# A two-layer product-quantised convolution block: where the sorts, the second image's preparation and the last image's pieces are placed

## The chip, the cores and the metric

The kernel runs on one core of a Trainium2 chip. A core has five engines, each with its own instruction stream: TensorE (PE, matrix multiplication, with weight loads listed as PEld), VectorE (DVE), ScalarE (ACT), GpSimd (POOL) and SyncE (SP, which here only issues DMA transfers; GpSimd issues transfers too). TensorE writes to PSUM, of which a partition has eight banks of 512 float32 numbers; the other engines work on SBUF, and VectorE and ScalarE also read PSUM. The metric is the time of one execution on the device, in microseconds (us); less is better.

## The reference

Sixteen images of 256 channels and 28 x 28 pixels go through one residual block. Each of its two convolutions is replaced by a soft lookup: for each channel the 3 x 3 neighbourhood of a pixel is compared with 16 codes, a softmax over the distances gives weights, and the weighted codes are multiplied by the convolution's weights.

```python
def amm_conv3x3(x, centroids, w_sub):
    patches = conv_general_dilated_patches(x, (3, 3), (1, 1), 'SAME')
    p = patches.reshape(B, C, s, Ho * Wo).transpose(0, 3, 1, 2)     # s = 9 taps
    d = sum(p * p, -1)[..., None] - 2.0 * einsum('bncs,cks->bnck', p, centroids) + sum(centroids ** 2, -1)
    attn = softmax(-d, axis=-1)                                      # k = 16 codes
    lut = einsum('cks,cso->cko', centroids, w_sub)
    return einsum('bnck,cko->bno', attn, lut)

xn = group_norm(x)                       # 32 groups
out = relu(bn1(amm_conv3x3(xn, centroids1, wsub1)))
out = bn2(amm_conv3x3(out, centroids2, wsub2))
out = out * sigmoid(relu(mean(out) @ w1 + b1) @ w2 + b2)             # squeeze and excitation
return x + relu(out + xn)
```

## The kernel before

**The pipeline.** An image takes two stages, one for each layer; the stages of neighbouring images are interleaved: (layer 0, image 0), (0, 1), (1, 0), (0, 2), (1, 1) and so on. A stage has 16 slots: two pixel tiles of 384 and 400 pixels (PXT), and for each 8 groups of channels. In a slot four steps of different groups run, each group passing through them slot by slot:

```python
patches(u, tile)   # SyncE: 4 DMAs, patch rows from DRAM (pat) to a tile pt, three slots ahead
logits(u)          # TensorE: 16 small matmuls into two pairs of PSUM banks
b_exp(u)           # ScalarE: exp of the logits, pair -> e
b_num(u)           # TensorE: 16 small matmuls, numerators and sum, e -> two pairs of banks
b_turn(u)          # VectorE: two 32x32 transposes pair -> nt, reciprocal of the sum
c_scale(u)         # GpSimd: numerators times reciprocal, nt -> k
c_turn(u)          # VectorE: transpose k -> q
c_look(u, o, h)    # TensorE: lookups, 128x128 weights on q, accumulated in the bank acc0 or acc1
```

The lookups of a pixel tile start four slots after its logits. Logits and numerators share a ring of three pairs of PSUM banks (`pair`); the lookups own two further banks. The first lookup runs in slot 4.

```python
    ring = [p_ring.tile([P, 2, 512], F32, name=f"pair{i}") for i in range(3)]
    def pair():
        turn[0] += 1
        return ring[turn[0] % 3]
    def bank():
        return pair()[:, 0]
```

**Jobs in a slot.** Everything else is put into slots by `plan.at(slot, position, function, ...)`. Positions within a slot, in order: LOGITS, LOAD, MOVE, EXP, LOOK_A, NUM, TURN, SMALL, LOOK_B, MAX, LOOK_C, TURN_BACK, REST. Each engine executes its instructions in the order in which they are so emitted; waits between engines are put in by the framework.

**The sorts.** Channels are put in another order by matmuls with a permutation, computed at the start. The first layer's lookup weights are sorted in six parts, the second layer's codes in one call, both with banks of the ring:

```python
    def sort_ws1(i):
        t = raw[i // 2][:, i % 2]
        for j in range(PART // P):
            ps = bank()
            for b in range(NB):
                nc.tensor.matmul(ps[:, :C], lhsT=t[:, b, j * P : (j + 1) * P], rhs=perm[:, b], ...)
            # copied to ws[0] by VectorE (j == 1) or ScalarE
    def by_position(ps, rhs):
        for v in range(NB):
            for b in range(NB):
                nc.tensor.matmul(ps[:, v], lhsT=perm[:, b, v * P : (v + 1) * P], rhs=rhs[:, b], ...)
    def sort_c2():
        ps = pair()
        m0 = 0
        for d, rhs in zip(d_c2, (c2_sb, c2_less)):
            m = rhs.shape[2]
            by_position(ps[:, :, m0 : m0 + m], rhs)
            t = scratch(NB * m).rearrange("p (b m) -> p b m", b=NB)
            nc.scalar.copy(t, ps[:, :, m0 : m0 + m])
            nc.gpsimd.dma_start(view(d, 0, [[m, P], [P * m, NB], [1, m]]), t)
            m0 += m
```

**Preparing an image.** The image is loaded, its statistics are taken (`gn_stats`, VectorE, four pieces), the group means follow (`gn_mean`, `gn_var`), the normalised image goes to `ims`, two copies shifted by a pixel (dx = 0 and 2; dx = 1 is the image itself) to `sides`, and from these the patch rows are written to DRAM: `to_pat`, one DMA for a shift, a block k of channels, a half h of the partitions, and optionally one pixel tile. Groups 0 to 3 of a stage read the half h = 0, groups 4 to 7 the half h = 1.

```python
        def prep_near(self, l, pat, t):
            for i, dx in enumerate((0, 2)):
                for k in range(NB):
                    self.at(t + i, REST, shift, l, dx, k)
            step = {v: i for i, v in enumerate(STEPS)}   # STEPS: h outermost, then dx in (1, 0, 2), then k
            put = lambda s, dx, k, h, px: self.at(s, REST, to_pat, l, step[dx, k, h], pat, *PXT[px])
            if l == 0:                                   # the second image only, with t = 10
                for i in range(len(STEPS)):
                    put(t + i // 2, *STEPS[i], 0)
                late = [(dx, k, h, 1) for dx in (0, 2) for h in range(2) for k in range(NB)]
                late += [(1, k, h, 1) for h in range(2) for k in range(NB)]
                for i, v in enumerate(late):
                    put(t + 6 + i // 2, *v)
                return
        # ... (layer 1)
        def norm(self, b, t):                            # the second image: t = 9
            for n, (k, i) in enumerate((k, i) for k in range(NB) for i in range(2)):
                self.at(t - 8 + n, REST, gn_stats, b, k, i)
            self.at(t - 3, SMALL, gn_mean, b)
            self.at(t - 1, SMALL, gn_var, b)
            for k in range(NB):
                self.at(t + k, REST, gn_apply, b, k)
```

The second image (b = 1) is loaded by SyncE in slot 0. Its first-layer stage is slots 16 to 31; slots 24 to 31 use the second pixel tile.

**The last image.** After its last lookup: the squeeze and excitation gate, then for two blocks k of channels and two halves i of the pixels y = relu(y * gate + normed) + x, and the stores.

```python
        def close_last(self, b, ob, te):
            # ... se_hidden, se_gate, se_scale
            for i in range(2):
                at(gate_norm, b, 0, i)        # VectorE: y * gate + normed
                at(relu, b, 0, i)             # ScalarE
                at(residual, b, 0, i)         # GpSimd: y + x
            for i in range(2):
                at(gate_norm, b, 1, i)        # VectorE
                at(relu_residual, b, 1, i)    # VectorE: max(y, 0) + x
            at(store_part, b, ob, 1, 0)
            at(store_part, b, ob, 0, 0, 2)
            at(store_part, b, ob, 1, 1)
```

Of the kernel before, what the change touches and what calls it, by code (L numbers as in the profile page):

```python
# [8 lines left out]
F32 = mybir.dt.float32  # L9
# [63 lines left out]
def kernel(  # L73
# [58 lines left out]

    def spare():

        return ring[(turn[0] + 1) % 3][:, 1]
# [53 lines left out]
    cw = [load(cw1, "cw0"), const.tile([P, NT, 32], F32, name="cw1")]  # L189
    load_codes = lambda: nc.sync.dma_start(cw[1], cw2)  # L190
# [134 lines left out]
    def sort_ws1(i):  # L325

        t = raw[i // 2][:, i % 2]
        for j in range(PART // P):
            ps = bank()
            for b in range(NB):  # L330
                nc.tensor.matmul(  # L331
                    ps[:, :C], lhsT=t[:, b, j * P : (j + 1) * P], rhs=perm[:, b], start=(b == 0), stop=(b == NB - 1)
                )
            w = ws[0][:, i * PART // P + j]
            if j == 1:
                nc.vector.tensor_copy(w, ps[:, :C])
            else:
                nc.scalar.copy(w, ps[:, :C])
# [3 lines left out]
    def by_position(ps, rhs):  # L342
        for v in range(NB):
            for b in range(NB):
                nc.tensor.matmul(  # L345
                    ps[:, v], lhsT=perm[:, b, v * P : (v + 1) * P], rhs=rhs[:, b], start=(b == 0), stop=(b == NB - 1)
                )

    def sort_c2():

        ps = pair()
        m0 = 0
        for d, rhs in zip(d_c2, (c2_sb, c2_less)):
            m = rhs.shape[2]
            by_position(ps[:, :, m0 : m0 + m], rhs)
            t = scratch(NB * m).rearrange("p (b m) -> p b m", b=NB)
            nc.scalar.copy(t, ps[:, :, m0 : m0 + m])
            nc.gpsimd.dma_start(view(d, 0, [[m, P], [P * m, NB], [1, m]]), t)
            m0 += m
# [213 lines left out]

    def gate_norm(b, k, i):

        y, gt = ys[b][0][half(k, i)], se[b]
        im = ims[0][:, k, W + i * (HW // 2) : W + (i + 1) * (HW // 2)]
        nc.vector.scalar_tensor_tensor(y, y, gt[:, k : k + 1], im, op0=ALU.mult, op1=ALU.add)

    def store_part(b, ob, k, i, n=1):  # L580
        v = slice(i * (HW // 2), (i + n) * (HW // 2))
        nc.sync.dma_start(ob[k * P : (k + 1) * P, v], ys[b][0][:, k, v])
# [179 lines left out]
    class Plan:  # L762
# [78 lines left out]
        def prep_near(self, l, pat, t):  # L841
# [6 lines left out]
            if l == 0:  # L848
                for i in range(len(STEPS)):
                    put(t + i // 2, *STEPS[i], 0)  # L850
                late = [(dx, k, h, 1) for dx in (0, 2) for h in range(2) for k in range(NB)]
                late += [(1, k, h, 1) for h in range(2) for k in range(NB)]
                for i, v in enumerate(late):
                    put(t + 6 + i // 2, *v)
# [13 lines left out]
        def norm(self, b, t):  # L868

            for n, (k, i) in enumerate((k, i) for k in range(NB) for i in range(2)):  # L870
                self.at(t - 8 + n, REST, gn_stats, b, k, i)
# [5 lines left out]
        def close_last(self, b, ob, te):  # L877
# [4 lines left out]
            for i in range(2):  # L882
                at(gate_norm, b, 0, i)
                at(relu, b, 0, i)
                at(residual, b, 0, i)
            for i in range(2):
                at(gate_norm, b, 1, i)
                at(relu_residual, b, 1, i)
            at(store_part, b, ob, 1, 0)
            at(store_part, b, ob, 0, 0, 2)  # L890
            at(store_part, b, ob, 1, 1)
# [55 lines left out]
    for si, (l, b) in enumerate(stages):  # L947
        t = si * NS
        plan.stage(l, b, pat_of(l, b), t, () if l == 0 else MAXED)
        if l == 0 and b >= 1:  # L950
# [5 lines left out]
            plan.norm(b, n0)  # L956
# [4 lines left out]
        if l == 1:  # L961
# [7 lines left out]
            else:  # L969
                plan.at(t + NS + LC - 1, REST, watch)  # L970
                plan.at(t + NS + LC - 1, REST, nc.gpsimd.drain)
                plan.close_last(b, out[b], t + NS + LC)
    for i in range(len(STEPS) // 2, len(STEPS)):
# [7 lines left out]
    plan.at(3, REST, load_codes)  # L981
    plan.at(3, REST, sort_c2)
# [116 lines left out]
```

## Time and profile before

| | |
|---|---|
| median of 3 runs | 2724.41 us (2719.69 to 2725.13) |
| span of the profiled run | 2720.5 us, mean granted TensorE clock 0.993 |
| instructions | 90148 |
| first logits | 30.92 us |
| first lookup (slot 4) | 62.61 us |
| last lookup | ends at about 2706.2 us |
| bytes moved by DMA | 514.98 MB, mean 189 GB/s |

How to read it. The page gives, for each engine, its busy time and its share of the span; then the span in 40 slices, with the busy share of each in tenths and the clock that TensorE was granted. The timeline lists instructions in order of time: start, length, engine, line of the kernel, operation, what it writes and reads, and how many were merged; in square brackets stands how long the engine was idle before it and what ended that. SPq is the queue in which SyncE issues DMA transfers: the time of such a line is the issue, and the data lands later. In a list of waits a line names the engine that waited, what it waited for, the sum in us, how often, and the longest.

A TensorE that is busy for a whole slice does not say that it does useful work at full speed[...].

### The profile page before, as it was taken

The page shows a single profiled execution, that of the slowest core. Times are in us where ns is not written, and L with a number is a line of the kernel's source. Part 1 is how long each engine was busy: PE and PEld are TensorE (multiplying, and loading weights), DVE is VectorE, ACT ScalarE, POOL GpSimd, SP SyncE. Part 2 cuts the span into 40 slices and gives each one's busy share as a digit, 9 for nine tenths or more (in the row PEclk, how much of TensorE's full clock was granted, in tenths as well). Part 3 has the DMA queues.
Part 4 walks back from the last instruction along what each step waited for, and adds up shares of the span by engine and source line. Part 5 has one row for each costly group of instructions (what it writes and reads, how often), then busy time and mean ns, then how long its engine had stood idle before and what let it go on. Part 6 is the DMA issues. An engine that isn't in the chain of part 4 may idle for free.

```text
span 2720.5 us, 90148 instructions
## 1 busy us (share of the span) xinstructions
PE 2684.0 (99%) x37748; PEld 1080.5 (40%) x37748; DVE 2177.3 (80%) x2639; ACT 1091.8 (40%) x1591; POOL 1905.0 (70%) x2723
## 2 busy tenths in 40 slices
PE   7999999999999999999999999999999999999997
PEld 4333434344343343433434343443443434333343
DVE  4668787887878878788787888878788787878886
ACT  2333443434334343433434334343443434334332
POOL 3888676766777677676776777667776776766764
PEclk8999999999999999999999999999999999999999
DMA  8688888767678676777767778676776767775561
GB/s 233 182 222 234 223 218 218 205 175 201 173 210 211 168 198 169 209 200 185 203 174 202 185 194 215 170 201 169 212 210 172 200 169 211 194 177 127 141 166 45
DMA packets 231944, 514.98 MB, mean 189 GB/s; under 512 B 34408, under 2 KB 186088, under 8 KB 231528
## 3 DMA queue, kind: packets, MB, share of 16 engines
q0 software_dynamic: 51968, 267.09, 37.0%
q1 hardware_dynamic: 179560, 242.03, 34.1%
q8 instruction: 299, 4.90, 0.7%
q14 instruction: 117, 0.96, 0.1%
HBM read 264.64 MB, written 244.37 MB: 187 GB/s over the span
## 4 chain that ended last, share of the span: by engine, by line
PE 97%; DMA 1%; DVE 1%; issue 0%; SPq 0%; ACT 0%; DVEq 0%
PE acc L729 63%; PE pair L603 17%; PE pair L665 16%; DMA pt<-pat 1%; PE pair L331 1%; PE pair L526 0%; DMA xt<-in_x 0%; DMA pt<-in_ws 0%; DMA sort_sb<-in_sorting 0%; PE pair L453 0%; PE pair L345 0%; PE pair L464 0%; PE pair L513 0%; DVE nt L677 0%; DVE y L555 0%
## 5 line engine op out<-in xcount | busy, mean ns | idle before, releaser
L729 PE MATMUL acc<-q,ws 128*128 128x384 f32 (+1 forms) x4096 | 1630.1, 518 | 0.0
L677 DVE STREAM_TRANSPOSE nt<-pair 128x832 f32<-128x832 f32 (+1 forms) x1024 | 977.5, 992 | 480.4 <-PE pair L665 382.2
L693 POOL TENSOR_TENSOR k<-nt,rc 128x832 f32<-128x832 f32 (+1 forms) x512 | 803.9, 1570 | 775.0 <-DVE rc L683 735.9
L655 ACT ACTIVATE e<-pair 128x768 f32<-128x768 f32 (+1 forms) x960 | 738.4, 821 | 1033.0 <-PE pair L603 1031.7
L729 PEld LDWEIGHTS acc<-q,ws 128*128 128x128 f32 x4096 | 701.2, 189 | 878.3 <-issue 542.1
L603 PE MATMUL pair<-pt,wd 19*32 19x384 f32 (+1 forms) x16384 | 498.1, 501 | 8.3 <-DVE nt L677 5.8
L711 DVE STREAM_TRANSPOSE q<-k 128x832 f32<-128x832 f32 (+1 forms) x512 | 488.6, 954 | 1.8 <-POOL k L693 1.8
L665 PE MATMUL pair<-e,cw 32*32 32x384 f32 (+1 forms) x16384 | 486.5, 500 | 0.2
L683 DVE RECIPROCAL rc<-nt 128x104 f32<-128x104 f32 (+1 forms) x512 | 398.5, 778 | 17.6
L603 PEld LDWEIGHTS pair<-pt,wd 19*32 19x32 f32 x16384 | 123.4, 103 | 303.3 <-issue 229.6
L699 POOL TENSOR_TENSOR tail<-nt,rc 128x104 f32<-128x104 f32 (+1 forms) x512 | 242.3, 473 | 0.0
L665 PEld LDWEIGHTS pair<-e,cw 32*32 32x32 f32 x16384 | 120.7, 103 | 288.8 <-issue 152.8
L729 PE MATMUL acc<-qt,ws 128*128 128x400 f32 (+1 forms) x512 | 217.0, 506 | 0.0
L705 POOL TENSOR_TENSOR total<-total,nt 128x96 f32<-128x96 f32 (+1 forms) x480 | 212.1, 442 | 0.0
L498 POOL DMA_DIRECT2D pat<-side x282 | 189.8, 673 | 1.2 <-ACT side L487 0.8
L705 POOL TENSOR_TENSOR total<-total,rc 128x96 f32<-128x96 f32 (+1 forms) x480 | 187.6, 391 | 0.0
L729 PEld LDWEIGHTS acc<-qt,ws 128*128 128x128 f32 x512 | 92.0, 189 | 94.7 <-issue 41.3
L648 ACT ACTIVATE e<-e 128x768 f32<-128x768 f32 (+1 forms) x64 | 54.7, 857 | 179.3 <-DVE e L641 178.3
L633 POOL TENSOR_TENSOR z<-z,mx 128x768 f32<-128x768 f32 (+1 forms) x64 | 98.8, 1544 | 0.0
L498 POOL DMA_DIRECT2D pat<-im x140 | 95.0, 679 | 0.1
L741 ACT ACTIVATE im<-acc,bnsh,bnsc 128x384 f32<-128x384 f32 (+1 forms) x64 | 43.4, 678 | 124.2 <-PE acc L729 124.2
L751 ACT ACTIVATE y<-acc,bnsh,bnsc 128x384 f32<-128x384 f32 (+1 forms) x64 | 43.4, 677 | 88.4 <-PE acc L729 85.7
(120 smaller groups left out, 894.4 us busy)
## 6 DMA issues: line engine op xcount, KB each, us to landing
pat<-side POOLq DMA_DIRECT2D x224, 588.0 KB, 5.7
pt<-pat SPq DMA_DIRECT2D x1024, 112.5 KB
pt<-pat SPq DMA_DIRECT2D x1024, 108.0 KB
pat<-im POOLq DMA_DIRECT2D x112, 588.0 KB, 5.3
xt<-in_x POOLq DMA_DIRECT2D x30, 784.0 KB, 6.8
out_dram<-y POOLq DMA_DIRECT2D x15, 784.0 KB, 5.8
pat<-side POOLq DMA_DIRECT2D x32, 300.0 KB, 5.9
pat<-side POOLq DMA_DIRECT2D x26, 288.0 KB, 5.3
```

What stands on the lines that cost most here:

```text
L498: eng.dma_start(view(pat, (ROWS * p0 + 9 * k + 3 * dx) * HW + px, [[ROWS * HW, m], [HW, 3], [1, n]]), bass.AP(v.tensor, v.offset, [list(v. ...
L603: nc.tensor.matmul(ps[t // 2][c : c + 32, t % 2, :n], lhsT=wd[l][32 * i : 32 * i + rows, 4 * u["m"] + t, :], rhs=u["pt"][32 * i : 32 * i + ...
L633: nc.gpsimd.tensor_tensor(z, z, mx.unsqueeze(2).to_broadcast(list(z.shape)), ALU.subtract)
L655: nc.scalar.activation(e[:, :, :n], ps[:, :, :n], AF.Exp, scale=2.0)
L665: nc.tensor.matmul(u["nm"][t // 2][32 * i : 32 * i + 32, t % 2, :n], lhsT=cw[l][c : c + 32, 4 * u["m"] + t, :], rhs=es[t // 2][c : c + 32, ...
L677: nc.vector.transpose(nt[:, :nb, 2 * v : 2 * v + 2].rearrange("p b t r -> p t b r"), ps[:, :, : 32 * nb].rearrange("p t (b r) -> p t b r", ...
L683: nc.vector.reciprocal(rc[:, : 8 * nb], u["nt"][:, :, SUM])
L693: nc.gpsimd.tensor_tensor(q[:, :nb].rearrange("p b (a s) -> p (b a) s", s=8), nt[:, :, :8], rc.unsqueeze(2).to_broadcast([P, 8 * nb, 8]), ...
L699: nc.gpsimd.tensor_tensor(tails[key][:, :nb, 8 * (m % 4) : 8 * (m % 4) + 8], nt[:, :, 8].rearrange("p (b a) -> p b a", a=8), rc.rearrange( ...
L705: nc.gpsimd.tensor_add(t[:, : 8 * nb], t[:, : 8 * nb], v)
L711: nc.vector.transpose(q[:, :, : 32 * nb].rearrange("p h (b r) -> p h b r", r=32), u.pop("k")[:, :nb].rearrange("p b (h r) -> p h b r", h=2),)
L729: nc.tensor.matmul(accs[key][:, :n], lhsT=ws[l][:, 2 * m + h if h < 2 else 2 * NQ + m // 4, o * P : (o + 1) * P], rhs=u["q"][h][:, :n], st ...
```

## The change

It has five parts. None changes what is computed.

- The sorts of the first layer's weights and the second layer's codes use the lookups' two banks, which have no other use before slot 4, and no longer pass through the ring. The sort of the codes is split into two calls, in slots 2 and 3. It is to keep the sorts from waiting on the ring and the ring from waiting on them.
- The first layer's code weights (cw0, 512 KB) are loaded later, behind the first patch loads and ahead of the second half's patch writes, to make room for what is needed first.
- The second image's statistics run in slots 3 and 4, two in each, where they ran one in each of slots 1 to 4: VectorE is not to meet them before the image has landed.
- The second image's patch writes go by half and by pixel tile, those that the next loads need first, and about one slot earlier.
- The last image's first piece is split over ScalarE and GpSimd (gate, addition, rectifier, addition), the other three pieces are VectorE's, and each piece has its store.

```diff
+    def free_bank(o):
+        return p_acc.tile([P, 512], F32, tag=f"acc{o}", name=f"acc{o}")
...
-    cw = [load(cw1, "cw0"), const.tile([P, NT, 32], F32, name="cw1")]
-    load_codes = lambda: nc.sync.dma_start(cw[1], cw2)
+    cw = [const.tile([P, NT, 32], F32, name=f"cw{l}") for l in range(2)]
+    def load_codes(l):
+        nc.sync.dma_start(cw[l], (cw1, cw2)[l])
...                                   # sort_ws1
-            ps = bank()
+            ps = free_bank((i + j) % 2)
...
-    def sort_c2():
-        ... (as above)
+    def sort_c2(i):
+        rhs, d = (c2_sb, c2_less)[i], d_c2[i]
+        m = rhs.shape[2]
+        t = scratch(NB * m).rearrange("p (b m) -> p b m", b=NB)
+        for v in range(NB):
+            ps = free_bank(v)
+            for b in range(NB):
+                nc.tensor.matmul(ps[:, :m], lhsT=perm[:, b, v * P : (v + 1) * P], rhs=rhs[:, b], ...)
+            nc.scalar.copy(t[:, v], ps[:, :m])
+        nc.gpsimd.dma_start(view(d, 0, [[m, P], [P * m, NB], [1, m]]), t)
...
+    def gate_only(b, k, i):           # ScalarE: y * gate
+    def add_norm(b, k, i):            # GpSimd: y + normed
...                                   # prep_near, l == 0
-                    put(t + i // 2, *STEPS[i], 0)
-                late = [(dx, k, h, 1) for dx in (0, 2) for h in range(2) for k in range(NB)]
-                late += [(1, k, h, 1) for h in range(2) for k in range(NB)]
+                    put(t + i // 3 if i < 6 else t - 1 + i // 2, *STEPS[i], 0)
+                late = [(dx, k, h, 1) for h in range(2) for dx in ((1, 0, 2), (0, 2, 1))[h] for k in range(NB)]
                 for i, v in enumerate(late):
-                    put(t + 6 + i // 2, *v)
+                    put(t + 5 + i // 2, *v)
...                                   # norm, with first = 3 for the second image
-                self.at(t - 8 + n, REST, gn_stats, b, k, i)
+                self.at(t - 8 + n if first is None else first + n // 2, REST, gn_stats, b, k, i)
...                                   # close_last
-            for i in range(2):
-                at(gate_norm, b, 0, i)
-                at(relu, b, 0, i)
-                at(residual, b, 0, i)
-            for i in range(2):
-                at(gate_norm, b, 1, i)
-                at(relu_residual, b, 1, i)
-            at(store_part, b, ob, 1, 0)
-            at(store_part, b, ob, 0, 0, 2)
-            at(store_part, b, ob, 1, 1)
+            at(gate_only, b, 0, 0)
+            at(add_norm, b, 0, 0)
+            at(relu, b, 0, 0)
+            at(residual, b, 0, 0)
+            for k, i in ((0, 1), (1, 0), (1, 1)):
+                at(gate_norm, b, k, i)
+                at(relu_residual, b, k, i)
+            for k, i in ((0, 1), (1, 0), (0, 0), (1, 1)):
+                at(store_part, b, ob, k, i)
...
+    plan.at(-1, REST, load_codes, 0)
...
-    plan.at(3, REST, load_codes)
-    plan.at(3, REST, sort_c2)
+    plan.at(3, REST, load_codes, 1)
+    for i in range(2):
+        plan.at(2 + i, LOOK_B, sort_c2, i)
```

## The prediction

> **What bounds the kernel now.** I read the page's first two parts, the waits of TensorE, and then the timeline around each of them.
>
> ```profile
> PE 2684.0 (99%) x37748; PEld 1080.5 (40%) x37748; DVE 2177.3 (80%) x2639; ACT 1091.8 (40%) x1591; POOL 1905.0 (70%) x2723
> ...
> PE   7999999999999999999999999999999999999997
> ```
>
> TensorE is busy for 99% of the span. Only the first and last of forty slices fall below 9, so a change that leaves the matmuls of the steady part alone can win only at the ends, or where a stall too short for these digits hides. I looked for such stalls in the starts of the logits (line 603) in TensorE's timeline. A slot is one tile of logits with its exponentials, numerators and lookups. In the steady part a group of ten lookups recurs at 382.93, 547.64 and 712.33 us in the chain of work: 164.7 us for 32 slots, 5.15 us a slot. Three intervals are far longer:
>
> - slot 3 begins at 45.90, slot 4 at 61.35: 15.45 us. Its work is one set of logits (0.86), one of numerators (0.86) and the sort of the second codes (2.23 + 2.50): 6.4 us. About 9 us are lost.
> - slot 17 begins at 130.23, slot 18 at 140.36: 10.13 us, 5.0 lost.
> - slot 25 begins at 175.89, slot 26 at 187.65: 11.76 us, 6.6 lost.
>
> The sum is 20.6 us, 0.76% of the time; after 190 us the windows show TensorE filled until 2640. The first loss, in the waits of TensorE and in the timelines of VectorE and TensorE:
>
> ```profile
> PE pair L603 <- DVE nt L677: 5.8, 2, 4.1
> PE pair L603 <- DMA pt<-pat: 2.5, 4, 1.1
> ```
>
> ```profile
> 51.53 0.57 DVE L446 BATCH_NORM_STATS2 gn_st<-xt 128x6 f32<-128x392 f32 x1 [8.58 <-DMA xt<-in_x]
> 52.02 1.83 DVE L677 STREAM_TRANSPOSE nt<-pair 128x768 f32<-128x768 f32 x2
> ...
> 53.04 1.53 PE L603 MATMUL pair<-pt,wd 19*32 19x384 f32 x16 [4.06 <-DVE nt L677]
> ```
>
> VectorE executes in order. It stands 8.58 us at the second image's first statistics until that image lands; the transpose that frees a PSUM pair is queued behind, and TensorE stands behind the transpose. A second effect is in the windows: the granted clock is 0.50 from 49 to 62 us, so the work after the stall runs at half speed (the sort of the codes takes 4.8 us).
>
> The other two losses begin at the DMA queue of SyncE:
>
> ```profile
> 119.12 1.39 SPq L589 DMA_DIRECT2D pt<-pat  x4
> ...
> 122.54 2.06 SPq L589 DMA_DIRECT2D pt<-pat  x4
> ...
> 164.54 1.39 SPq L589 DMA_DIRECT2D pt<-pat  x4
> ...
> 167.53 6.14 SPq L589 DMA_DIRECT2D pt<-pat  x4
> ...
> 178.54 2.72 PE L603 MATMUL pair<-pt,wd 19*32 19x400 f32 x28 [1.08 <-DMA pt<-pat]
> ```
>
> The loads for slots 16, 17, 24 and 25 should be issued three slots ahead. In the waits of that queue from 100 to 180 us, 21.4 us go to the second image's patches (11.8 on the shifted copies, 9.6 on the image itself). The load of slot 24 needs the last pixel tile's image rows, which are last in the order (GpSimd issues them at 159.34). So slot 25's load leaves at 167.5 to 173.7 and TensorE needs it at 175.89.
>
> **What the Trainium skill says.** "TensorE: Matmul & The Clock Gate", section "What's actually happening": after an idle window of about 3.4 us the array's clock falls to half, and sustained activity restores it. The trace agrees: a 4.06 us wait, then 0.50 granted; 0.50 again from 180 to 185. "DMA: Bandwidth & Descriptors", section "Issuing engines are not separate DMA queues": transfers of SyncE and GpSimd run on the same 16 engines and interleave. The page of before agrees, with 37.0% and 34.1% of those engines for the two queues; so moving a transfer earlier can delay another. "SBUF — State Buffer", section "SBUF: two separate sides": VectorE with two SBUF inputs and GpSimd share a port pair as an exclusive lock. In the last 20 us two GpSimd additions take 2.52 us where two elsewhere take 1.98, and a fused VectorE operation beside them 1.26 against 0.57. I read that as the same thing.
>
> **The change part by part.**
>
> 1. Statistics in slots 3 and 4, where they ran in slots 1 to 4. The order of VectorE's instructions puts them behind the transposes of slot 3's numerators, which the image's landing (51.53) then no longer holds up. I walk slots 2 to 5 with TensorE warm. Sorting starts about 0.5 us earlier: its first part waits 2.31 us on the code correction for a ring bank, and the permutation itself is done only at 19.83, against a start at 20.35. The ring stops passing sort copies, which took another 0.6 us before slot 2. So slot 2 begins near 42. Logits 0.9, numerators 1.4 (the second pair waits for an exponential), first code sort 2.2: slot 3 at 46.5. Its patches landed at 48.0 before and I expect the same, so logits end at 49, numerators at 50.4, the second code sort (2.5) at 53, and slot 4 begins at 53 where it was 61.35: 8.4 us earlier.
>
> 2. The sorts use the lookups' two banks, free until slot 4. They number the same 72 and 16 rows, so none of the 18.4 + 4.8 us of matmul time leaves; only ring waits do, counted in 1. Two copies to the scratch tile become four. The order of ScalarE's instructions shows a cost: the second sort's copy waits for the DMA that empties the first sort's scratch. GpSimd issues that after slot 2's scaling, near 49.5, and before, such a transfer took 8.1 us to land. ScalarE would be held to about 57, with slot 4's exponentials behind it. Slot 4 then ends near 60 and not 58: I take 2.4 off, leaving 6 us of gain at slot 5.
>
> 3. The first layer's code weights (512 KB) leave the start of the queue and go behind twelve patch loads. From 10 to 18 us the DMA share is 1.05 or more and from 24 to 32 it is 0.28 to 0.62, so the first patches come perhaps 1.5 us earlier (estimate: 512 KB at 336 GB/s). But slot 0 waits behind sorts anyway, and from 34 to 42 the share is again 1.0, where the 512 KB now fall. I book 0 for it; the weights are needed near 37.5, issued near 31.
>
> 4. Patches by half and pixel tile: the six transfers that gate slot 16 go in slots 10 and 11 (they were in 10 to 12), and those that gate slot 24 in 15 to 17 (they reached into slot 20). One slot is 5 us and the load of slot 16 was some 5 us late; three slots are 15 us and the load of slot 24 was 9 late. Both gates should open. I take 4.5 of 5.0 and 5.5 of 6.6, since the bytes are unchanged and the DMA share there is 0.87 to 0.91: earlier patches meet other loads.
>
> 5. The last image. Before, six VectorE operations and two GpSimd additions run from 2709.14 to 2714.03. Now VectorE still has six (three gates, three rectified sums), ScalarE a gate (0.63, from the same gate in the other images) and a rectifier (0.5), GpSimd again two additions. With the shared port two of the six take 1.26: 4 x 0.57 + 2 x 1.26 = 4.8 us, against 4.9. The last store leaves at the same time: 0.
>
> Sum: 6 + 4.5 + 5.5 = 16. I take off 1 us for waits that earlier slots create where transfers are dense, giving 15: 2724.4 - 15 = 2709.
>
> **Rivals.** *The DMA engines become the bound at slots 5 to 9.* They moved 8.1 MB from 40 to 75 us; compressed to 28 us that asks 289 GB/s, about what full slices show (270 at a share of 0.92). For it: shares of 1.0 around 48 and 60 to 66. Against: loads run three slots ahead and TensorE waited for none there. It would return 4 of the 6 us: 2713. *ScalarE's hold is longer* (landing after 60, or GpSimd late): it replaces VectorE's wait almost wholly, TensorE cools again, and part 1 yields 2 us: 2713; with the DMA rival 2717. *The stalls of slots 17 and 25 only move* a slot or two, because it was bandwidth and not the gate: against it stand the 21.4 us of queue waits on patches; it would leave 6 us of gain: 2718. *All three stalls vanish with the cold clock*: 20.6 us and a little from the sorts, 2702.
>
> **Range and chances.** The centre is 2709. The rivals singly give 2713 to 2718, the best case 2702; three runs before spread over 5.4 us. So 2701 to 2718 for eight in ten. Two per cent is 54 us. TensorE's idle and cold time does not hold that much, so faster by over 2% has 0.01, and slower by over 2% would need new stalls of 54 us in a part that has not been altered: 0.01.
>
> **What would show it.** Right: no wait of VectorE on the image above 1 us; slot 4 at 52 to 55 us; granted clock above 0.9 from 53 to 62; intervals at slots 17 and 25 below 6 us; last rectified sum within 0.5 us of its distance from the last lookup before (8 us). For part 2: a ScalarE wait of some microseconds at the second code copy, in slot 3. Wrong: slot 5 later than 63 (the hold, or patches, took the place of the image), logits waiting on patch loads for over 2 us between slots 5 and 32, or a numerator of slot 0 waiting for its code weights.

## The result and the profile after

| | before | after |
|---|---|---|
| median | 2721.55 us (2719.69 to 2725.13, 6 runs) | 2711.70 us (2710.84 to 2714.00, 6 runs) |
| span of the profiled run | 2720.5 us | 2709.6 us |
| mean granted clock | 0.993 | 0.996 |

The ratio is 0.9963, with a 95% interval of 0.9950 to 0.9976: 9.9 us, where 15 were predicted. The first two parts of the page of after, in the rows that were shown of before:

```profile
PE 2676.7 (99%) x37748; PEld 1076.6 (40%) x37748; DVE 2177.7 (80%) x2639; ACT 1092.8 (40%) x1593; POOL 1906.4 (70%) x2723
...
PE   7999999999999999999999999999999999999997
```

TensorE's busy time fell by 7.3 us, with as many matmuls as before (37748): part of the gain is time that counted as busy, matmuls at the lower clock or waiting for data among them. The forty digits do not differ at all. As before, the change can only be seen in the starts of the slots (start of the logits' first matmul, us from the start of the span):

| slot | before | after | gained so far |
|---|---|---|---|
| 0 | 30.9 | 28.8 | 2.2 |
| 1 | 37.9 | 39.0 | -1.1 |
| 2 | 43.3 | 44.4 | -1.1 |
| 3 | 45.9 | 48.3 | -2.4 |
| 4 | 61.4 | 54.0 | 7.4 |
| 5 | 66.4 | 64.0 | 2.4 |
| 16 | 125.4 | 123.1 | 2.3 |
| 17 | 130.2 | 127.9 | 2.3 |
| 18 | 140.4 | 133.4 | 7.0 |
| 25 | 175.9 | 168.4 | 7.5 |
| 26 | 187.7 | 176.1 | 11.6 |
| end of the last lookup | 2706.2 | 2694.9 | 11.3 |

So 4.7 us were won at slot 17 and 4.1 at slot 25, both from the patches' order, and only 2.4 before slot 5, where 6 were expected. Slot 4 itself begins 7.4 us earlier and then gives 5.0 back. TensorE's waits in after (sum, times, longest), the five rows that touch the change:

```profile
PE pair L616 <- DVE nt L690: 1.7, 1, 1.7
PE pair L616 <- DMA pt<-pat: 1.7, 3, 0.9
PE acc L338 <- DVE sort_sb L313: 1.4, 1, 1.4
PE pair L678 <- ACT e L668: 1.2, 1, 1.2
PE acc L742 <- ACT scratch L360: 0.9, 1, 0.9
```

Of the 5.8 us on VectorE's transposes 1.7 are left, which lie after 200 us and were there before: the wait of 4.1 us behind the image is gone. Those on patches went from 2.5 to 1.7. The sorts no longer wait on the ring, as part 2 intended: in before they waited 2.3 and 0.5 us for its banks, here 1.4 us for the permutation itself (L338). And a new row has come: lookups (L742) that wait for ScalarE's copy (L360) of a bank. TensorE's timeline through slot 4, with the sort of the codes ahead of it (L357), and ScalarE's timeline beside it:

```profile
52.70 1.35 PE L357 MATMUL acc<-c_less,sort_sb 128*128 128x160 f32 x8
53.98 0.83 PE L616 MATMUL pair<-pt,wd 19*32 19x384 f32 x2
55.42 2.32 PE L616 MATMUL pair<-pt,wd 19*32 19x384 f32 x30 [0.61 <-DMA pt<-pat]
58.60 2.62 PE L742 MATMUL acc<-q,ws 128*128 128x384 f32 x4 [0.87 <-ACT scratch L360]
61.15 1.46 PE L678 MATMUL pair<-e,cw 32*32 32x384 f32 x32
62.55 1.56 PE L742 MATMUL acc<-q,ws 128*128 128x384 f32 x4
64.03 0.93 PE L616 MATMUL pair<-pt,wd 19*32 19x384 f32 x32
```

```profile
58.26 0.49 ACT L360 COPY scratch<-acc 128x160 f32<-128x160 f32 x2 [5.72 <-DMA dc<-scratch]
58.63 1.53 ACT L668 ACTIVATE e<-pair 128x768 f32<-128x768 f32 x2
```

Three things follow one another in the 10.0 us of this slot. The patches are late: the logits end at 57.74 where 0.93 us would have ended them at 54.9. ScalarE stands 5.72 us for the DMA that empties its scratch tile, so the bank is not copied and the first lookups wait to 58.60; of the hold only 0.87 us is seen, because the late patches hide the rest. Then the array is cold: four lookups take 2.62 us and a set of numerators 1.46, where the same rows a little later take 1.56 and 0.93. These terms are 2.8, 0.9 and 1.6 us, and account for what the slot has above a steady one (10.0 less 5.15 is 4.9; neighbouring rows overlap by about 0.1 us each).

The windows show what surrounds this. Columns: the stretch; length; busy time of each engine with its instructions; then the granted clock, the DMA share and GB/s:

```profile
32.00:34.00 2.00, 2.00 (x17) 1.51 (x5) 0.00 (x0) 1.51 (x2) 0.00 (x0) 0.50 0.85 183
...
60.00:62.00 2.00, 2.00 (x34) 0.35 (x33) 0.00 (x0) 0.16 (x1) 1.07 (x2) 0.50 0.87 251
```

The cold stretch of before (49 to 62 us) is now only some 59 to 62 us, but a new one stands at 32 to 35, where before had 1.00. Of the sixteen such rows from 34 to 66 us thirteen have a DMA share of 0.9 or more.

### The profile page after: what moved, and what is told of

Its sections match the earlier page's. It is cut to its first block, busy times and chain, and to the rows that moved or that the text cites. A ratio compares the mean times of both kernels' runs of the same rounds, so it can differ in the third digit from the quotient of the medians.

```text
span 2709.6 us, 90142 instructions
## 1 busy us (share of the span) xinstructions
PE 2676.7 (99%) x37748; PEld 1076.6 (40%) x37748; DVE 2177.7 (80%) x2639; ACT 1092.8 (40%) x1593; POOL 1906.4 (70%) x2723
## 4 chain that ended last, share of the span: by engine, by line
PE 95%; POOL 2%; DMA 1%; DVE 1%; issue 0%; ACT 0%; SPq 0%; DVEq 0%; ACTq 0%; POOLq 0%
PE acc L742 62%; PE pair L616 16%; PE pair L678 16%; POOL k L706 1%; POOL pat L500 1%; PE acc L338 0%; PE pair L528 0%; POOL total L718 0%; DMA pat<-side 0%; DMA ws<-in_wsub,src 0%; POOL ws L410 0%; DMA dc<-scratch 0%; PE pair L466 0%; PE pair L515 0%; PE pair L455 0%
## 5 line engine op out<-in xcount | busy, mean ns | idle before, releaser
L742 PE MATMUL acc<-q,ws 128*128 128x384 f32 (+1 forms) x4096 | 1628.4, 517 | 0.9 <-ACT scratch L360 0.9
L742 PEld LDWEIGHTS acc<-q,ws 128*128 128x128 f32 x4096 | 700.1, 189 | 878.0 <-issue 540.4
L742 PE MATMUL acc<-qt,ws 128*128 128x400 f32 (+1 forms) x512 | 217.0, 506 | 0.0
L742 PEld LDWEIGHTS acc<-qt,ws 128*128 128x128 f32 x512 | 92.0, 189 | 94.7 <-issue 41.3
```

The lines of the kernel that those rows point to most:

```text
L742: nc.tensor.matmul(accs[key][:, :n], lhsT=ws[l][:, 2 * m + h if h < 2 else 2 * NQ + m // 4, o * P : (o + 1) * P], rhs=u["q"][h][:, :n], st ...
```

## The experiments

Twelve kernels, each beside runs of before on the same chip (median of before there 2722.4 to 2723.2 us). The first theory: ScalarE's hold is what gives back the gain of slot 4. Its rivals: the patches of slots 3 and 4 are late by themselves, because the first layer's code weights now lie ahead of them in a stretch where the DMA engines are full; or parts 1 to 3 do nothing and all comes from the patches' order.

### own_scratch: the hold taken away

After, with a tile of another pool for the sorted codes, so that the second copy waits for no transfer.

```diff
-        t = scratch(NB * m).rearrange(...)
+        t = tpool.tile([P, 832], F32, tag="z", name="c2_out")[:, : NB * m].rearrange(...)
```

> The changed kernel, but each code sort copies to a tile of its own (an idle buffer of another pool) and not to the shared scratch. Theory (ScalarE is held 5.7 us by the transfer that empties the first sort's scratch, and the lookups of slot 4 behind it, because they need the bank that ScalarE still has to copy): the wait of ScalarE on the transfer is gone, slot 5 begins near 59.5 us where it was 64.0, and the whole is 4 to 5 us shorter, about 2707. Rival (the patches of slots 4 and 5 land late in any case): slot 5 begins at 62 or later with waits on patch loads, and the whole gains under 2 us.

Measured: 2713.42 us, ratio 0.9969 (0.9956 to 0.9981). The hold is gone, as ScalarE's timeline shows; but TensorE's timeline has slot 5 at 66.16, later than in after:

```profile
54.80 0.29 ACT L360 COPY c_out<-acc 128x160 f32<-128x160 f32 x1 [2.23 <-PE acc L357]
```

```profile
57.03 0.83 PE L616 MATMUL pair<-pt,wd 19*32 19x384 f32 x2 [0.59 <-DMA pt<-pat]
58.80 1.57 PE L616 MATMUL pair<-pt,wd 19*32 19x384 f32 x26 [0.94 <-DMA pt<-pat]
```

The copy now waits only for its matmuls. The logits of slot 4 come in pieces as their patches land, until 60.4, and the four lookups behind them take 2.93 us, cold all the same. The theory (slot 5 near 59.5) fell: in after the hold was one of two waits that ended at nearly the same time. That slot 5 became later, and not merely no earlier, is not shown: apply_later and tail_undone below have the program of after up to there, and in their profiles slot 5 begins at 66.4 and 64.1.

### apply_later: the wait that became visible at slot 25

In after slot 25 still takes 7.7 us. ScalarE's timelines of after and then of before, at that place:

```profile
171.94 1.04 ACT L479 ACTIVATE im<-xt,gn_nb,gn_rstd 128x784 f32<-128x784 f32 x1 [5.66 <-POOL gn_nb L474]
```

```profile
180.06 1.04 ACT L477 ACTIVATE im<-xt,gn_nb,gn_rstd 128x784 f32<-128x784 f32 x1 [6.30 <-POOL gn_nb L472]
```

ScalarE waits for GpSimd's factors of the third image, with the exponentials of slot 25 queued behind it. The wait was in before as well, and TensorE was then waiting for patches. The experiment is after with that normalisation two slots later.

```diff
-                self.at(t + k, REST, gn_apply, b, k)
+                self.at(t + k + (2 if b == 2 else 0), REST, gn_apply, b, k)
```

> The changed kernel, but the third image is normalised two slots later (slots 26 and 27, not 24 and 25). Theory (what is left of the stall of slot 25 is ScalarE standing 5.7 us at that image's normalisation, because GpSimd comes late to its factors): the interval of slot 25 falls from 7.7 to about 5 us and the whole by 2.7 us, to about 2709. Rival (slot 25 still waits for its patches, which land at about the same time): the interval stays above 7 us, with a wait of the logits on a patch load.

Measured: 2713.30 us, 0.9965 (0.9953 to 0.9978). Slot 25 falls from 7.7 to 5.7 us, and slots 28 and 29, where ScalarE now waits for patch writes, rise from 7.4 to 8.8. ScalarE's waits from 170 to 200 us:

```profile
ACT im L754 <- DMA pat<-im: 5.9, 2, 5.5
```

In after this row is 0.5. From slot 24 over the next sixteen sets of logits this kernel needs 80.0 us and after 80.2: nothing is won. Up to slot 24 the program is that of after, and yet the lookups of slot 4 waited 2.4 us for the bank, not 0.9, and slot 5 began at 66.4, not 64.0: the start itself scatters by more than 2 us.

### patches_only: part 4 alone

Before, with nothing but the new order of the second image's patch writes (the diff of `prep_near` above).

> The kernel before, with the new order of the second image's patch writes alone. Theory: the interval of slot 17 falls from 10.1 to 5 us as in the changed kernel; that of slot 25 falls from 11.8 to 7 to 8 us, the rest being ScalarE's wait on the third image's factors; 8 to 9 us shorter, about 2713. Rival (the order helps only because earlier slots were already ahead): under 5 us.

Measured: 2712.88 us, 0.9962 (0.9948 to 0.9976): the whole of the gain of after, whose ratio is 0.9963. In its profile slot 17 takes 6.3 us (from 10.1), slot 25 takes 7.5 (from 11.8), but slot 18 takes 6.9 (from 4.8), because its own patches are late. TensorE's timeline there:

```profile
137.49 0.92 PE L603 MATMUL pair<-pt,wd 19*32 19x384 f32 x26 [1.02 <-DMA pt<-pat]
```

### stats_only: part 1 alone

Before, with the second image's statistics in slots 3 and 4.

```diff
-                self.at(t - 8 + n, REST, gn_stats, b, k, i)
+                self.at(t - 8 + n if first is None else first + n // 2, REST, gn_stats, b, k, i)
...
-            plan.norm(b, n0)
+            plan.norm(b, n0, 3 if b == 1 else None)
```

> The kernel before, with the second image's statistics in slots 3 and 4 alone. Theory: VectorE's wait of 8.6 us on the image is gone. The code sort in slot 3 still takes a pair of the ring and is copied by ScalarE between its two halves, but there is no hold by a transfer; slot 4 begins at about 55 to 57 us (61.4 before), slot 5 at about 61, 4 to 6 us shorter: more than the 2.4 us that slot 5 gains in the changed kernel. Rival (the gain at slot 4 needs the lookups' banks): slot 4 at 59 or later, under 3 us.

Measured: 2720.97 us, 0.9993 (0.9984 to 1.0001, 12 runs), and not the 4 to 6 us shorter that were expected. VectorE's wait for the image is gone, slot 4 begins at 55.4 (from 61.4) and slot 5 at 63.5 (from 66.4). TensorE's timeline in slot 4:

```profile
57.21 0.92 PE L603 MATMUL pair<-pt,wd 19*32 19x384 f32 x26 [0.94 <-DMA pt<-pat]
```

Without part 2 and without part 3 the patches of slot 4 are late too, and by slot 26 (186.6, before 187.7) most of the 2.9 us had gone again: the two patch stalls, still there, wait for transfers and not for TensorE.

### sorts_only: part 2 alone

Before, with the sorts in the lookups' banks and the code sort in two calls (the diff of `free_bank`, `sort_ws1` and `sort_c2` above).

> The kernel before, with the sorts in the lookups' banks alone (code sort in two calls). Theory: VectorE still stands at the second image, so slot 4 begins at about 58 (the sort of the first codes moves ahead of the stall, 2.2 us) and slot 5 at about 64; then the patches' gates of slots 17 and 25 take most of it back: whole 0 to 2 us shorter. Rival (the ring was a bound of its own): slot 5 before 62, whole over 3 us shorter.

Measured: 2729.24 us, 1.0022 (1.0010 to 1.0033): slower by 6 us. The timelines of TensorE, ScalarE, GpSimd and VectorE:

```profile
65.27 2.93 PE L727 MATMUL acc<-q,ws 128*128 128x384 f32 x4 [7.32 <-ACT scratch L356]
```

```profile
64.92 0.49 ACT L356 COPY scratch<-acc 128x160 f32<-128x160 f32 x2 [9.76 <-DMA dc<-scratch]
```

```profile
54.34 1.51 POOL L691 TENSOR_TENSOR k<-nt,rc 128x768 f32<-128x768 f32 x1 [5.53 <-PE pair L601]
...
56.92 0.79 POOL L357 DMA_DIRECT2D dc<-scratch  x1
```

```profile
51.09 0.57 DVE L444 BATCH_NORM_STATS2 gn_st<-xt 128x6 f32<-128x392 f32 x1 [6.54 <-DMA xt<-in_x]
```

Read from the last to the first. VectorE stands at the image until 51.09 and only then transposes and inverts for GpSimd's scaling, which ends near 56.9. (The profile names a TensorE instruction as what ended GpSimd's 5.53 us; the reciprocal that the scaling reads ends at 54.18 on VectorE.) Only behind the scaling does GpSimd issue the transfer of the first sorted codes; it releases the scratch tile 8.0 us later, at 64.92; only then is the bank copied, and the lookups wait 7.32 us. In after the same transfer is issued at 51.88 and the copy starts at 58.26. So part 2 puts the lookups behind a chain that begins with the image; part 1 is what takes the image out of it. That is read from the two traces: no run has these two parts and no others.

### codes_first: part 3 undone

After, with the first layer's code weights loaded at the start again.

```diff
-    cw = [const.tile([P, NT, 32], F32, name=f"cw{l}") for l in range(2)]
+    cw = [load(cw1, "cw0"), const.tile([P, NT, 32], F32, name="cw1")]
...
-    plan.at(-1, REST, load_codes, 0)
```

> The changed kernel, but the first layer's code weights are loaded at the start again, as before. Theory (their 512 KB now lie in the full stretch from 34 us, ahead of the patches of slot 3): those patches land 1.3 to 2 us earlier, slot 4 begins at 52 to 53 (54.0), slot 0's logits no later than in the kernel before (30.9); slot 5 gains at most 1.5 us, because ScalarE's hold stays; the whole the same within 1.5 us. Rival (their place at the start held up the first patches): slot 0's logits begin 1.5 us later or more than in the changed kernel and finish later, and the whole is 1.5 us longer or more.

Measured: 2711.29 us, 0.9961 (0.9947 to 0.9975), the same as after. Now the hold bites alone. TensorE's timeline:

```profile
53.93 1.58 PE L616 MATMUL pair<-pt,wd 19*32 19x384 f32 x32
61.11 2.92 PE L742 MATMUL acc<-q,ws 128*128 128x384 f32 x4 [5.60 <-ACT scratch L360]
```

No wait on patches stands in slots 3 and 4 (the logits of slot 4 end at 55.5, in after at 57.7), and the lookups wait 5.60 us for the bank; slot 5 begins at 66.8 (64.0 to 66.4 in the three profiles with the start of after). This is the mirror image of own_scratch: there the patches ended last, here the hold.

### codes_own and codes_own_late: both waits taken away

The two edits together; and then also the second layer's code weights (512 KB) in slot 9 and not slot 3.

```diff
-    plan.at(3, REST, load_codes, 1)
+    plan.at(9, REST, load_codes, 1)
```

> The changed kernel with both: own tiles for the code sorts, and the first layer's code weights at the start. Theory (at slot 4 two causes stand side by side, the patches that the code weights delay and the scratch that a transfer has to empty; each alone hides the other, which is why removing one gained nothing): slot 5 begins at 58.5 to 60.5 us, where it was 64.0 in the changed kernel and 66.2 and 66.8 with one of the two; slot 6 may then wait on patches. The whole 2 to 5 us shorter than the changed kernel, 2707 to 2710. Rival (a third cause at the same place): slot 5 after 63, whole 2711 or more.

> The same, and the second layer's code weights (512 KB) in slot 9 and not in slot 3. Theory (after slot 5 the transfers are the bound until about 70 us, as slot 6 showed where only the image was moved back): slots 5 to 7 pass with no wait on patches above 0.5 us, slot 8 begins at 74 to 76 (80.9 minus 5 to 6), and the whole is 5 to 6 us shorter than the changed kernel, about 2706. Rival: the wait moves on again to slots 6 to 9 and the whole stays at 2709 or more.

Measured: codes_own 2711.60 us, 0.9962 (0.9951 to 0.9974). Slot 4 begins at 52.7 as it should, but its patches are late again, now with no hold beside them, and slot 5 begins at 63.9, as the rival had it:

```profile
56.04 1.58 PE L616 MATMUL pair<-pt,wd 19*32 19x384 f32 x26 [1.36 <-DMA pt<-pat]
```

codes_own_late, 2711.27 us, 0.9958 (0.9941 to 0.9974): slot 5 begins at 59.1 and slot 6 at 65.0, and slot 6 then takes 9.8 us on late patches. Slot 8 begins at 80.2, where 74 to 76 were expected and after has 80.9.

### room: the other way to clear slot 4

own_scratch, with the second image loaded in slot 2 and not slot 0, its statistics in slots 4 and 5, and the first image's patch writes for the second pixel tile a slot later.

```diff
-                plan.at(0, REST, load_x, b, x[b], nc.sync)
+                plan.at(2, REST, load_x, b, x[b], nc.sync)
...
-            plan.norm(b, n0, 3 if b == 1 else None)
+            plan.norm(b, n0, 4 if b == 1 else None)
...
-        plan.at(1 + i // 3 if i < 6 else i // 2, REST, to_pat, 0, i, d_pat[0], *PXT[1])
+        plan.at(2 + i // 3 if i < 6 else 1 + i // 2, REST, to_pat, 0, i, d_pat[0], *PXT[1])
```

> The changed kernel with own tiles for the code sorts, and with two kinds of transfers that nobody needs soon moved back: the second image's load (784 KB) from slot 0 to 2, its statistics to slots 4 and 5, and the first image's patch writes of the second pixel tile (six of 300 KB first) one slot later. Theory (from 34 to 66 us the DMA engines are full, and this bounds slots 3 to 5 once the engines' waits are gone): 1.7 MB less lie ahead of the patches of slots 4 and 5, 5 to 6 us at 300 GB/s; slot 5 begins at 58 to 61 us (66.2 with own tiles alone, 64.0 in the changed kernel), with under 1 us of waits on patch loads. Of that 2 to 5 us reach the end. Rival (latency of the small loads, not the fill of the engines): slot 5 stays at 63 or later.

Measured: 2714.87 us, 0.9971 (0.9964 to 0.9978, 20 runs). Slot 5 begins at 58.4, as the theory had it, and two slots later TensorE stands as it stood in slot 4. Its timeline, and the windows of this kernel (columns as above):

```profile
65.83 0.83 PE L616 MATMUL pair<-pt,wd 19*32 19x384 f32 x2 [0.93 <-DMA pt<-pat]
67.56 1.57 PE L616 MATMUL pair<-pt,wd 19*32 19x384 f32 x26 [0.90 <-DMA pt<-pat]
```

```profile
48.00:52.00 4.00, 3.49 (x66) 1.35 (x68) 2.56 (x4) 1.80 (x4) 2.49 (x4) 1.00 0.62 138
...
60.00:64.00 4.00, 4.00 (x42) 1.61 (x41) 3.97 (x8) 0.96 (x2) 3.89 (x6) 1.00 1.04 375
```

The transfers taken out of 44 to 52 us (share near 0.6) came back at 56 to 64 at 375 GB/s, and slot 6 took 12.7 us. Slot 8 began at 81.8, and of the 2 to 5 us expected at the end none arrived.

### tail_undone: part 5 undone

After, with `close_last` of before: first block gated by VectorE, rectified by ScalarE and added by GpSimd, three stores.

> The changed kernel with the last image's pieces as before. Theory: from the last lookup to the last rectified sum 7.9 to 8.1 us in both, the whole within 0.5 us of the changed kernel. Rival (the split of the first piece gains): 1 us longer or more.

Measured: 2711.66 us, 0.9962 (0.9948 to 0.9976), against 0.9963: no difference.

### all_four and ring_start: the removals put together

all_four is codes_own_late with the third image's group means a slot earlier, so that ScalarE does not wait for its factors in slot 25. ring_start is all_four with the sort of the lookup weights back in the ring.

```diff
-            self.at(t - 3, SMALL, gn_mean, b)
-            self.at(t - 1, SMALL, gn_var, b)
+            self.at(t - (4 if b == 2 else 3), SMALL, gn_mean, b)
+            self.at(t - (2 if b == 2 else 1), SMALL, gn_var, b)
```

```diff
-            ps = free_bank((i + j) % 2)
+            ps = bank()
```

> The same, and the third image's group means and variances one slot earlier (slots 20 and 22), its normalisation where it was (24 and 25). Theory (ScalarE stands 5.7 us at that normalisation because GpSimd is late with the factors; moving the normalisation later met a patch write of the second image instead): the interval of slot 25 falls from 7.7 to about 5 us, that of slot 28 to 29 stays at 7.4 for two, and 2 to 2.7 us more are won: about 2703.5. Rival (another wait takes its place): slot 26 gains under 1 us.

> The last one (own tiles for the code sorts, both code weights moved, the third image's factors earlier), but the first layer's weights are sorted in the ring's banks again, as before. Theory (in the lookups' banks the sorts bring TensorE to slot 0 at 28.8 us, where it idles for patches that land near 31, and in most runs its clock falls to 0.50 for 2 to 6 us; in the ring it arrives with the patches): slot 0 begins at 30.9 and slot 1 at 37.5 to 38.2 us in this run, where the runs with the lookups' banks had 37.5 to 40.8; granted clock 1.00 from 28 to 40; the whole 1 to 3 us shorter than those, 2707 to 2710, with less spread. Rival (a later wait takes it, as it took all the others): 2711 or more.

Measured: all_four 2712.92 us (2708.60 to 2716.06), 0.9964 (0.9950 to 0.9979). Slot 25 takes 5.4 us (from 7.7) and slots 28 and 29 take 8.4 (from 7.4). ring_start 2710.71 us (2707.72 to 2712.96), 0.9953 (0.9940 to 0.9967). Its slot 0 begins at 31.1, slot 1 at 37.6, and the clock is 1.00 from 28 to 40 us, as the theory of the start said; slot 8 begins at 80.2. Each local wait went where it was meant to go, and neither kernel can be told from after: the intervals overlap.

## Why the prediction was right, and where not

**The bound and the three stalls: right.** The range of 2701 to 2718 us holds 2711.7. The gain sits at the three places that were named, and at no other: after slot 26 nothing more is won or lost (11.6 us there, 11.3 at the end). That the time came within 2.7 us of the centre, 2709, is partly luck: the centre was 2724.4 less 15; the gain came out 5 us smaller, and the six runs of before have their median at 2721.55, 2.9 us lower.

**Part 1 less part 2, "leaving 6 us of gain at slot 5": the term that was mis-sized.** It measured 2.4 us in the profile of after and 0.0 and 2.3 in the two others with the same start (apply_later, tail_undone), and in the times parts 1 to 3 and 5 together add nothing that can be seen: patches_only has 0.9962, after 0.9963, each known to about 0.0014 or 4 us. The mechanism of part 1 was right: VectorE no longer waits for the image, and its statistics run as one row at 55.47 us. So was that of part 2: ScalarE was held to 58.3, where about 57 was predicted (the transfer was issued at 51.88 and not 49.5, but took 6.4 us and not 8.1). Five things were off, and one reading of the clock:

- The walk to slot 2. "Slot 2 begins near 42": it began at 44.4, later than before, although the sorts were indeed done earlier. TensorE reached slot 0 at 28.75, 2.2 us earlier and not 0.5 (in before the clock stood at 0.50 from 21.3 to 24.7 under the first sort, here it did not), and its logits trickled until 32.2 as their patches landed; then the clock was 0.50, and the 24 sort matmuls of slot 0 took 6.86 us in place of the 5.5 of a warm start.
- The patches of slot 3. "I expect the same" landing, 48.0: its last logits began at 50.4, and the four loads were issued at 41.79 in place of 40.47. This is rival one, DMA engines as the bound, but at slots 3 and 4 and not 5 to 9. The code weights' new place may be part of it, as codes_first suggests; but codes_own has them at the start too, and there the patches of slot 4 are late until 57.6. So their place does not settle it.
- Slot 4, which was to end 2.4 us late behind ScalarE's hold. It was 5 us late, by patches (2.8), hold (0.9) and cold clock (1.6). Rival two had this size ("part 1 yields 2 us", with TensorE cold again), but from the hold alone. The prediction also had the wrong link: it let the hold reach TensorE through the exponentials, while TensorE stops at the lookups, which need the bank that ScalarE has not copied (7.32 us in sorts_only). That the sorts' banks are "free until slot 4" was true of the lookups' use and not of the sorts' own reader.
- The removal of one wait was counted as gain. own_scratch, codes_first and codes_own take away the hold, the late code weights, and both; slot 5 began at 66.2, 66.8 and 63.9, against 64.0. At slot 8, which begins at 83.3 in before and 80.9 in after, these three stand at 83.1, 83.6 and 80.8; but apply_later, with the start of after, has 83.3, so these differences are about as large as the scatter of one program. The earliest of all variants, all_four at 78.2, has a median no lower than that of after.
- The code sorts. The walk was to be "with TensorE warm", but its 2.2 and 2.5 us for the two code sorts are the times of the cold stretch of before; in after they took 1.25 and 1.35. That slot 4 came at 54.0, so near the predicted 53, is two errors that nearly cancel: the second sort began 2.3 us later (52.7 in place of 50.4, behind the patches of slot 3) and took 1.15 us less.

The reading is "a 4.06 us wait, then 0.50 granted". In before the clock fell at 48.6 us, ahead of that wait (48.98 to 53.04), behind half a set of logits that took from 45.90 to 48.98 as its patches landed. TensorE's timeline of before, and the window that holds the fall:

```profile
48.01 0.97 PE L603 MATMUL pair<-pt,wd 19*32 19x384 f32 x10 [0.47 <-DMA pt<-pat]
```

```profile
48.00:50.00 2.00, 0.97 (x10) 0.16 (x10) 0.00 (x0) 0.81 (x1) 0.00 (x0) 0.66 1.04 355
```

So the image's wait kept the clock low, but it was the thin matmuls before it that brought it down, and taking that wait away did not keep the array warm.

Part 2 was credited with a better start. Alone it costs 6 us (sorts_only), so the change holds one part that harms by itself and that part 1, by the traces, makes nearly harmless.

**Part 3, booked at 0: right** in the sum (codes_first). "First patches perhaps 1.5 us earlier" was wrong: their loads left at 25.76 in place of 25.96, and the logits of slot 0 ended at 32.2 in place of 32.4. So the room that the 512 KB left at the start brought nothing; that they fall into the full stretch from 34 us the prediction had named, at no cost.

**Part 4, 4.5 + 5.5 us: right in the mechanism, and near in size.** In after slot 17 gave 4.7. Slot 25 gave 4.1: the gate opened, and a wait of ScalarE that had lain behind it (6.30 us in before, 5.66 in after) kept the rest. The prediction looked only at the wait that TensorE named there. In the profiles this is 8.8 us; alone, part 4 gave 9.5 (patches_only, 2712.88 against 2722.37; by the interval 6.5 to 14). The queue shows the gate. SyncE's waits from 100 to 180 us in after, and its loads for slots 24 and 25:

```profile
SPq L602 <- DMA pat<-side: 7.6, 5, 2.7
```

```profile
152.39 1.50 SPq L602 DMA_DIRECT2D pt<-pat  x4
156.49 2.36 SPq L602 DMA_DIRECT2D pt<-pat  x4
```

The first line is all that is left of 21.4 us on patches; the row on the image itself is gone, and the two loads leave 12 and 11 us earlier than in before (164.54 and 167.53). Rival three, that these stalls only move, came true in part. Slot 18, steady in before (4.8 us) and in after (4.9), takes 7.1 us in tail_undone, which has the same program up to there, and 6.9 in patches_only, late patches in both: over slots 16 to 18 the gain is 4.6, 2.4 and 1.7 us in these three. That slot 18 gave nothing back in after was luck. At slot 25 the rival holds only for what apply_later and all_four tried to add: there slots 28 and 29 took back 1.4 of 2.0 and 1.0 of 2.3 us.

**Part 5, 0: right** (tail_undone). From the gate to the last rectified sum 5.01 us, before 4.89. The port shared by VectorE and GpSimd that was read from before is there again. VectorE's timeline, and GpSimd's beside it:

```profile
2698.94 1.37 DVE L583 SCALAR_TENSOR_TENSOR y<-y,se_gt,im 128x392 f32<-128x392 f32 x1
2700.35 0.57 DVE L569 SCALAR_TENSOR_TENSOR y<-y,xt 128x392 f32<-128x392 f32 x1
```

```profile
2698.57 1.32 POOL L591 TENSOR_TENSOR y<-y,im 128x392 f32<-128x392 f32 x1 [8.06 <-ACT y L587]
```

The addition (1.32 us) meets the first of these two fused operations, which takes 1.37 us; the one after it, which begins with GpSimd at rest, takes 0.57.

**The signs named beforehand.** Came true: no wait on the image, slot 4 at 52 to 55 (54.0), slot 17 below 6 us (5.5), the hold in slot 3, the last rectified sum (7.9 us behind the last lookup, before 7.8). Failed: slot 5 not later than 63 (64.0), clock above 0.9 from 53 to 62 (0.50 at 60), slot 25 below 6 us (7.7). No logits of after wait on a patch load between slots 5 and 32. The numerators of slot 0 waited for their code weights in one variant only, 0.9 us in own_scratch.

**What stays open.** Between 34 and 66 us the DMA share is near 1.0 for most of the time and the waits change places whatever is removed. Whether the bytes themselves or their order sets the end there was not separated: no run left bytes out. Nor is it settled what of the scatter from slot 2 to slot 8 comes from the clock and what from transfers; that of slot 1 follows the clock (last section). Part 4 both reorders the writes and moves them about a slot earlier, and no run has one without the other.

## What to carry to other kernels

Before counting a wait as gain, look for what else ends within a few microseconds of it, on every engine that feeds the same instruction: here the hold, the patches and the third image's factors each stood behind the wait that the profile named. Where the DMA engines are full, moving transfers moves waits; where a queue only stands behind the wrong transfer, as at slots 17 and 25, writing the same bytes in another order and somewhat earlier wins most of it. And try the parts of a change singly: one of five made the gain, three did nothing measurable alone or undone, and one cost 6 us by itself.

## What was not expected of the hardware

**To arrive early can cost.** Ten profiled kernels have the sorts in the lookups' banks. In nine TensorE began the logits of slot 0 at 28.7 to 28.9 us, ahead of part of their patches, and in eight of these the granted clock then fell to 0.50 for 3.4 or 6.8 us. In the four kernels with these sorts in the ring, as in own_scratch, the clock had been at 0.50 for 3.4 us earlier, from about 21 us, under the first sort; slot 0 began at 30.9 to 31.3 (own_scratch 30.2), and the clock stayed at 1.00 from 28 to 40 us. The sort of slot 0 in all_four (clock 1.00) and in codes_own_late (0.50):

```profile
31.95 5.64 PE L338 MATMUL acc<-sort_sb,pt 128*128 128x256 f32 x24
```

```profile
32.84 8.04 PE L338 MATMUL acc<-sort_sb,pt 128*128 128x256 f32 x24
```

The same section of "TensorE: Matmul & The Clock Gate" that the prediction named says that the window of activity runs freely, so that where it falls differs from run to run. That fits a start which differs by up to 3 us between these kernels (slot 1 at 37.5 to 40.8), and a clock that fell in codes_own_late and not in all_four, although their programs are the same up to there. The traces show the grid: in each profile all changes of the granted clock lie whole multiples of 3.41 us apart (in after 31.65, 35.07, 58.96, 62.37). In the eight kernels a step of this grid fell at 30.9 to 32.5 us, in the last 2 us of the thin logits or just behind them, and the clock dropped there. Where it stayed low for one step slot 1 began at 39.0 to 39.4, for two at 40.6 to 40.8. In all_four, reckoned back from a change at 56.66, the steps fell at 29.4 and 32.8; the clock did not drop, and slot 1 began at 37.5, as in the kernels with the ring (37.6 to 38.0). But no single idle time of 3.4 us stands in the trace: the matmuls only came thinly, 32 in 3.2 to 4.1 us. How thin is thin enough was not measured.

**A small transfer holds its buffer long.** The scratch tile with the sorted codes, 144 KB, came free 6.4 us (after), 7.3 (codes_first) and 8.0 (sorts_only) after the issue of its transfer began. In after the DMA share was 0.90 meanwhile; no run has this transfer where the engines are at rest, so what part of it their fill makes is not shown.
